# A decoder block on one core: the recurrent cell's first operand beside the last latent unit, and expert inputs by scattered rows

## The chip, the cores and the metric

One core of a Trainium2 chip runs one program, a whole decoder block. The metric is the device time of one execution in microseconds (us), the median of several runs. All data are float32, apart from a few bfloat16 helpers. PE is the matrix engine, DVE, ACT and POOL the three engines that work on rows, SP the engine whose queue issues most loads.

## The reference, cut to what matters

The input x has 2 batch entries of 1024 rows with 256 columns. Six layers follow one another: linear attention with a feed-forward part, latent cross-attention, a recurrent cell, causal self-attention with 16 heads, cross-attention to 64 context rows, and a mixture of experts. The change touches the seams of the cell and of the experts.

```python
# recurrent cell: scans over the two batch entries, 1024 rows each
def step(c, xt):
    ft = sigmoid(xt @ wf.T + c @ uf.T + bf)
    it = sigmoid(xt @ wi.T + c @ ui.T + bi)
    gt = tanh(xt @ wc.T + c @ uc.T + bc)
    return ft * c + it * gt, None
c_final, _ = lax.scan(step, c0, x)          # c0 = in_c, the same for every row
h = tanh(einsum('tbi,oi->tbo', x, wo) + c_final @ uo.T + bo)
...
x = x + cell(layernorm(x))
x = x + causal_attention(layernorm(x))
x = x + cross_attention(layernorm(x), context)
x = x + experts(layernorm(x))
```

The experts' layer takes 8 groups of 256 rows. Each row goes to its two best experts of 8, into one of 64 places that each expert has in each group; a row that finds no place is dropped. An expert computes `gelu(v @ w0) * (v @ w1) @ wo` on its 8 x 64 rows, with a hidden width of 1368, and each row's output is the sum of its two experts' rows weighted by the gates.

## The kernel before, in words

The residual x stays in SBUF as 16 tiles of 128 rows. Matmuls need operands with features on the partitions, so each layer normalises rows (statistics on DVE, the reciprocal root `rs_y` on POOL, the application on DVE at line L183), transposes the result on PE, and copies it out of PSUM on DVE or ACT. Layers are separate stages on PE. Inside most stages the order of instructions is written by hand (generators that are advanced in turn, or a list of step names like `CROSS_ORDER`); each engine then executes its own instructions strictly in that order. A few stages are ordered by a scheduler instead.

**Latent attention.** Four units (two of each batch entry) are attended one after another in 18 steps each. `Latent.run` advances, in each step, the attention of unit u (`attend`) and one step of a side generator (`side`). With unit 2 the side generator is `finish(0)`; unit 3 has none. PSUM holds three score buffers `s` of 128x1024 here. After unit 3 comes `finish(1)`, which ends with the output matmuls (L1046) and the additions to x (L1054).

**Recurrent cell.** `recurrent_cell` normalises all four groups of 512 rows (`norm_rows`, transposes at L192, copies at L123 and L125), then makes the bias of the first step's gates, `gb`: as the start state is the same vector `in_c` for every row, its product with each gate's matrix is one column (12 matmuls 128x1 at L1137, additions at L1144). Then come the gates of scan step 0 (L1158, 24 matmuls of 512 columns), those of step 1, and the output projection of each row tile, the second half beside the start of causal attention.

**Cross-attention.** `CROSS_ORDER` interleaves four units of 512 rows (`norm`, `turn`, `proj`, `max`, `sc`, `exp`, `os`, `out`, ...) with the routing of units 0 to 2 (`route_...`: statistics of x, normalised rows xn, transposes at L2062, router product at L2070), with the choice of experts for batch entry 0 (`choose_0`), and with four of the one-hot matrices (`ones`). The routing of unit 3 and `choose` for batch entry 1 follow in `Experts.run_in`.

**Experts.** In `run_in` rows are dispatched with matmuls: for each group of 256 rows, DVE makes for each 128-row tile a one-hot matrix `dm` of 128x512 (8 experts x 64 places, L2158 and L2159), and PE multiplies the rows xn with it (L2206, 64 records of 512 columns). ACT and DVE copy the results (L2215, L2219) into `pair`, the operands of all eight experts. Then each expert runs 11 chunks of hidden columns (`hidden`: 8 records each at L2266, gelu on ACT at L2274, product on DVE at L2275) and its output matmuls (L2281). Outputs of experts 0 to 5 are stored to rows in DRAM (`eo_rows`) and gathered later by 32 indirect transfers of POOL's queue (L2299) beside the last two experts; outputs of experts 6 and 7 are combined by matmuls with `cT`. Weights w0 and w1 (`load`) and wo (`load_out`) of an expert come by SP's queue, two experts ahead and at the expert's start.

## Time and the profile before

| what | us |
|---|---|
| median of 3 runs (1740.96 to 1742.96) | 1742.32 |
| the profiled execution | 1744.03 |
| its span on the core | 1742.2 |
| PE busy | 1657.0 |
| DVE, ACT, POOL busy | 807.3, 515.3, 263.5 |
| end of the latent outputs to the first gate record | 575.2 to 596.43 |
| gates of step 0 | 596.43 to 621.56 |
| cross-attention's last output matmuls end | 1225.7 |
| first up record of expert 0 | 1273.44 |
| gather transfers on POOL, 32 | 31.7 busy |

The profile is of one execution; its own time is that of its span and 1.8 us around it. A row of PE's timeline gives start, length and number of records of a run of matmuls, and in brackets the idle time ahead of it with what ended that. One logical float32 matmul leaves two records.

### The profile page before, as it was taken

The numbers are of one execution on the slowest core, as the hardware profiler recorded it, in microseconds if no ns is written. First come the engines' busy times: TensorE is split into PE (matmuls) and PEld (weight loads), VectorE is DVE, ScalarE is ACT, GpSimd is POOL, SyncE is SP. The second block draws the span as 40 slices with busy tenths as digits, with TensorE's granted clock in tenths as the row PEclk, the third lists the DMA queues.
The fourth block names the chain that finished last, engine by engine and source line by source line (L and its number), as shares of the span: only waits on it lengthen the run. The fifth ranks groups of instructions, "written<-read, shape, count | busy, mean of one in ns | idle before, by whom it ended". The sixth has DMA issues, their size and how long they took to land. (4 is left out here: it accounts for less than half of the span.)

```text
span 1742.2 us, 20929 instructions
## 1 busy us (share of the span) xinstructions
PE 1657.0 (95%) x8679; PEld 873.8 (50%) x8686; DVE 807.3 (46%) x1458; ACT 515.3 (30%) x872; POOL 263.5 (15%) x294
## 2 busy tenths in 40 slices
PE   7998899999999799999999999888899999999998
PEld 5746454343433547433433433556546655665466
DVE  8515237556542424476667668367621221111332
ACT  2321331432234123245555455433121111111110
POOL 2001140441223101113111112220000000000420
PEclk9999999999999799989999999999899999999999
DMA  6000000000000100100000000130003311332321
GB/s 230 1 3 1 0 3 1 1 0 1 1 1 0 36 1 1 32 1 1 1 2 1 1 1 2 53 146 2 1 0 109 108 66 45 109 109 71 101 67 49
DMA packets 30549, 59.15 MB, mean 34 GB/s; under 512 B 3640, under 2 KB 23672, under 8 KB 30072
## 3 DMA queue, kind: packets, MB, share of 16 engines
q1 hardware_dynamic: 25512, 50.46, 8.4%
q0 software_dynamic: 1536, 4.20, 0.9%
q10 hardware_dynamic: 3408, 3.17, 0.5%
q8 instruction: 68, 1.11, 0.3%
q14 instruction: 25, 0.20, 0.0%
HBM read 51.00 MB, written 6.82 MB: 33 GB/s over the span
## 5 line engine op out<-in xcount | busy, mean ns | idle before, releaser
L2266 PE MATMUL ps_s<-pair,w 128*128 128x512 f32 (+1 forms) x704 | 304.8, 592 | 0.2 <-ACT pair L2215 0.2
L2266 PEld LDWEIGHTS ps_s<-pair,w 128*128 128x128 f32 (+1 forms) x704 | 130.9, 187 | 164.4 <-issue 163.3
L1455 ACT ACTIVATE pT<-ps_t 128x512 f32<-128x512 f32 (+3 forms) x344 | 150.7, 490 | 145.3 <-PE ps_t L1420 143.0
L1345 PE MATMUL ps_s<-kT,qT 32*128 32x512 f32 (+3 forms) x768 | 178.1, 553 | 11.2 <-DVE part L1361 7.2
L2275 DVE TENSOR_TENSOR hid<-ga,ps_s 128x512 f32<-128x512 f32 (+1 forms) x88 | 60.5, 687 | 272.7 <-ACT ga L2274 272.7
L1420 PE MATMUL ps_t<-qT,kT 32*128 32x512 f32 (+3 forms) x688 | 181.8, 547 | 2.2 <-ACT pT L1455 2.2
L2281 PE MATMUL ps_o<-wo,hid 128*128 128x256 f32 (+1 forms) x704 | 153.6, 379 | 0.0
L1361 DVE TENSOR_REDUCE part<-ps_s 128x2 f32<-128x1024 f32 (+3 forms) x128 | 130.5, 1024 | 43.6 <-PE ps_t L1420 37.3
L2281 PEld LDWEIGHTS ps_o<-wo,hid 128*128 128x128 f32 (+1 forms) x704 | 133.8, 190 | 22.0 <-issue 4.1
L2274 ACT ACTIVATE ga<-ps_s 128x512 f32<-128x512 f32 (+1 forms) x88 | 52.5, 597 | 246.5 <-PE ps_s L2266 246.4
L1345 PEld LDWEIGHTS ps_s<-kT,qT 32*128 32x128 f32 x768 | 59.8, 189 | 87.0 <-issue 43.6
L1027 ACT ACTIVATE pT<-ps_s 128x1024 f32<-128x1024 f32 x64 | 65.5, 1024 | 115.9 <-PE ps_s L1020 115.9
L1385 PE MATMUL ps_o<-pT,vr 128*32 128x256 f32 (+4 forms) x1408 | 97.9, 356 | 1.8 <-POOL pT L1413 1.5
L1413 POOL TENSOR_SCALAR_AFFINE_SELECT pT<-pT 128x256 f32<-128x256 f32 x128 | 52.0, 408 | 313.3 <-ACT pT L1455 305.6
L2299 POOL DMA_INDIRECT found<-eo_rows,index x32 | 31.7, 992 | 422.7 <-DMA eo_rows<-rows 388.1
L915 DVE TENSOR_REDUCE part<-ps_s 128x2 f32<-128x1024 f32 x64 | 76.4, 1218 | 28.4 <-PE ps_s L908 27.7
L1353 DVE TENSOR_TENSOR ps_s<-ps_s,causal 128x256 f32<-128x256 f32 x128 | 55.0, 430 | 63.7 <-PE ps_t L1420 42.9
L1032 POOL TENSOR_TENSOR acc<-acc,pT 128x1024 f32<-128x1024 f32 x24 | 59.4, 2477 | 160.0 <-ACT pT L1027 157.3
L1385 PEld LDWEIGHTS ps_o<-pT,vr 128*32 128x32 f32 x1408 | 28.8, 108 | 97.9 <-issue 84.0
L1420 PEld LDWEIGHTS ps_t<-qT,kT 32*128 32x128 f32 x688 | 69.7, 188 | 10.7 <-ACT pT L1455 7.0
L908 PE MATMUL ps_s<-kT,qT 64*128 64x512 f32 x256 | 71.5, 639 | 0.8 <-DVE part L898 0.6
L947 PE MATMUL ps_o<-pT,vr 128*64 128x512 f32 x256 | 68.9, 619 | 0.9
(387 smaller groups left out, 2254.7 us busy)
## 6 DMA issues: line engine op xcount, KB each, us to landing
w<-in_w SPq DMA_DIRECT2D x32, 684.0 KB, 7.3
wo<-in_wo SPq DMA_DIRECT2D x8, 1280.0 KB, 6.8
eo_rows<-rows ACTq DMA_DIRECT2D x12, 256.0 KB, 4.6
w_ffn<-in_w_ffn SPq DMA_DIRECT2D x1, 2304.0 KB, 14.8
x<-in_x SPq DMA_DIRECT2D x4, 512.0 KB, 4.9
w<-in_w_cell SPq DMA_DIRECT2D x2, 1024.0 KB, 16.5
out_x<-x SPq DMA_DIRECT2D x8, 256.0 KB, 2.2
w<-in_w_lat SPq DMA_DIRECT2D x2, 768.0 KB, 16.2
```

Of the source, the lines that this page charges most:

```text
L908: nc.tensor.matmul(s3[:, hh, :], lhsT=q[rows, qt * P : (qt + 1) * P], rhs=kt[rows, half * 512 : (half + 1) * 512], start=True, stop=True,)
L915: nc.vector.tensor_reduce(part[:, half, qt, :], s3, AX.X, ALU.max, negate=True)
L947: nc.tensor.matmul(self.o[hh * 64 : hh * 64 + 64, :], lhsT=self.vr[b][:, kk, h * 64 : (h + 1) * 64], rhs=pT[:, hh, :], start=first, stop=last,
L1027: nc.scalar.activation(pT, s3, AF.Exp)
L1345: nc.tensor.matmul(s3[:, hh, :n], lhsT=q[rows, qt * P : (qt + 1) * P], rhs=kt[rows, at : at + n], start=True, stop=True,)
L1361: nc.vector.tensor_reduce(out, s3[:, :, :n], AX.X, ALU.max, negate=True)
L1385: nc.tensor.matmul(self.o[hh * 32 : hh * 32 + 32, cols], lhsT=vr[:, kk, 4 * grp + hh, :], rhs=pts[hh // 2][:, hh % 2, cols], start=first, ...
L1420: nc.tensor.matmul(out, lhsT=kt[rows, kk * P : (kk + 1) * P], rhs=q[rows, j * 512 + q0 : (j + 1) * 512], start=True, stop=True,)
L1455: nc.scalar.activation(pT[:, hh, q0:], heads[hh][:, q0:], AF.Exp)
L2266: nc.tensor.matmul(s[:n, i * 512 : (i + 1) * 512], lhsT=wt[:, kc, at : at + n], rhs=v[:, kc, :], start=(kc == 0), stop=(kc == DC - 1),)
L2275: nc.vector.tensor_mul(hid[:n, hc, :], ga[:n], s[:n, 512:])
L2281: self.k.nc.tensor.matmul(o, lhsT=hid[:n, hc, st * P : (st + 1) * P], rhs=to[:n, hc, :], start=(hc == 0), stop=(hc == len(HCH) - 1),)
```

## The change

**Cell.** `recurrent_cell` becomes a class. The operand of batch entry 0 (the norms of groups 0 and 1) and `gb` are made by `cell.ahead()`, which is the side generator of latent unit 3. `gb` is made in another form: six matmuls with `in_c` as the stationary side give one row of 768, ACT copies it out, and six matmuls 1x1 turn it back into columns. The norms of groups 2 and 3 are steps beside the gates of scan step 0.

**Experts.** Only experts 0 and 1 are still dispatched with matmuls, with one-hot matrices of 128 columns (`ones`, `disp`, and ACT copies `put`). Those of batch entry 0 are in `CROSS_ORDER`. For experts 2 to 7, POOL's queue scatters the rows of xn with 32 indirect transfers to rows in DRAM, which SP's queue fills with zeros beforehand (8 transfers of 393 KB behind those of `eo_rows` and ahead of wo of expert 0). For each of these experts, POOL's queue fetches its rows with 8 transfers of 64 rows, and 8 transposes and an ACT copy (`turned`) make the operand, ahead of the output matmuls of the expert before. Expert 0's up matmuls run in two halves of 256 columns. The first half, which needs batch entry 0 alone, is interleaved by hand (`FIRST_ORDER`) with the routing of unit 3, `choose` of batch entry 1 and its dispatch; the second half follows.

**Cross order.** `CROSS_ORDER` is another list of the same steps, with the new ones merged in.

```diff
-    def run(self, late):
+    def run(self, late, following):
...
+            if u == 3:
+                side = following
...
-def recurrent_cell(k, x, wt, pool):
-    xT = pool.tile([P, DC, B * N], F32, tag="xT", bufs=1, name="xT")
-    for g in range(NT // 4):
-        xh = norm_rows(k, pool, x, g)
-        k.feature_major(lambda i: xh[:, i, :], xT[:, :, g * 512 : (g + 1) * 512])
-    gb = pool.tile([P, 3, DC], F32, tag="gb", bufs=1, name="gb")
...
                 nc.tensor.matmul(
-                    o[:, 0:1],
-                    lhsT=w[u][:, kc, mc * P : (mc + 1) * P],
-                    rhs=k.vec("in_c", kc),
-                    start=(kc == 0),
-                    stop=(kc == DC - 1),
-                )
-            nc.vector.tensor_add(gb[:, gi, mc : mc + 1], o[:, 0:1], k.vec(bias, mc))
...
+class Cell:
...
+    def norm(self, g):
+        k, nc = self.k, self.k.nc
+        rows = lambda i: self.x[:, 4 * g + i, :]
+        mv, r = k.ln_stats(rows, 4)
+        yield
+        xh = self.rows()
+        for i in range(4):
+            k.ln_apply(xh[:, i, :], rows(i), mv, r, i)
+        yield
+        s = k.s()
+        for kc in range(DC):
+            for i in range(4):
+                at = (kc * 4 + i) * P
+                nc.tensor.transpose(s[:, at : at + P], xh[:, i, kc * P : (kc + 1) * P], k.ident)
+        dst, half = self.xT[g // 2], g % 2 * 512
+        nc.vector.tensor_copy(dst[:, 0, half : half + 512], s[:, :512])
+        nc.scalar.copy(dst[:, 1, half : half + 512], s[:, 512:])
+        yield
+    def first(self):
...
+        row = self.rows().rearrange("p t d -> p (t d)")[0:1, : 3 * D]
+        s = k.s()
+        for gi, (_, u, _) in enumerate(self.GATES):
             for kc in range(DC):
                 nc.tensor.matmul(
+                    s[0:1, gi * D : (gi + 1) * D], lhsT=k.vec("in_c", kc), rhs=self.w[u][:, kc, :],
+                    start=(kc == 0), stop=(kc == DC - 1),
+                )
+        nc.scalar.copy(row, s[0:1, : 3 * D])
+        yield
+        s = k.s()
+        for i in range(3 * DC):
+            nc.tensor.matmul(
+                s[:, i : i + 1], lhsT=row[:, i * P : (i + 1) * P], rhs=k.ones_row[:, 0:1], start=True, stop=True
+            )
+        self.gb = self.pool.tile([P, 3, DC], F32, tag="gb", bufs=1, name="gb")
+        at = VEC["bf"][0]
+        nc.vector.tensor_add(
+            self.gb.rearrange("p g m -> p (g m)"), s[:, : 3 * DC], k.vecs[:, at : at + 3 * DC]
+        )
+        yield
+    def ahead(self):
+        yield from self.first()
+        for g in range(2):
+            yield from self.norm(g)
...
-                    pairs = [(w[wn], xT[:, kc, step * N + nb * 512 : step * N + (nb + 1) * 512], kc) for kc in range(DC)]
+                    pairs = [(w[wn], self.xT[step][:, kc, cols], kc) for kc in range(DC)]
...
-        state = new
-        if step == 0:
-            continue
-        for t in range(NT):
-            rows = slice((t % TB) * P, (t % TB + 1) * P)
-            lhs = [xT[:, c, t * P : (t + 1) * P] for c in range(DC)] + [state[:, c, rows] for c in range(DC)]
-            o = k.t()[:, :D]
-            for c, a in enumerate(lhs):
-                nc.tensor.matmul(
-                    o, lhsT=a, rhs=w["uo" if c >= DC else "wo"][:, c % DC, :], start=(c == 0), stop=(c == len(lhs) - 1)
-                )
-            h = pool.tile([P, D], F32, tag="h", bufs=3, name="h")
-            nc.vector.tensor_add(h, o, k.row("cell_bo"))
-            nc.scalar.activation(h, h, AF.Tanh)
-            nc.vector.tensor_add(x[:, t, :], x[:, t, :], h)
-            yield t == TB - 1
+    def scan(self, pool):
+        self.xT[1] = self.operand(pool)
+        self.rows = lambda: pool.tile([P, 4, D], F32, tag="xh", bufs=2, name="xh")
+        side = chain(self.norm(2), self.norm(3))
+        for n, _ in enumerate(self.gates(pool, 0, None)):
+            next(side, None)
+        drain(side)
+        drain(self.gates(pool, 1, self.state))
...
+route_xT_1 sc_21 rows_3 route_prod_1 exp_21 route_copy_1 sc_31 choose_0 choose_0 sum_2 exp_31 choose_0
+choose_0 inv_2 spr_2 choose_0 val_2 choose_0 os_2 yT_2 choose_0 sc_30 choose_0 out_2 exp_30 ones_03
+ones_02 ones_01 ones_00 disp_00 add_2 route_stat_20 sum_3 put_00 ones_07 ones_06 ones_05 val_3 inv_3
+ones_04 spr_3 os_3 route_stat_21 disp_01 yT_3 route_mean_2 put_01 out_3 route_root_2 route_norm_20
+route_norm_21 add_3 route_turn_2 route_xT_2 route_prod_2 route_copy_2
...
-            elif name == "ones":
-                moe.ready[args[0]] = moe.dispatch(args[0])
+            elif name in ("ones", "disp", "put"):
+                getattr(moe, name)(*args)
...
+FIRST_ORDER = """
+up_06 route_stat_30 up_08 gelu_06 route_stat_31 route_mean_3 mul_06 route_root_3 gelu_08 mul_08 up_04
+route_norm_30 route_norm_31 route_turn_3 gelu_04 mul_04 route_xT_3 route_prod_3 up_01 route_copy_3
+choose_1 choose_1 choose_1 gelu_01 choose_1 up_00 choose_1 mul_01 choose_1 gelu_00 mul_00 up_0a choose_1
+choose_1 up_05 gelu_0a ones_12 ones_13 up_07 gelu_05 ones_10 ones_11 mul_0a gelu_07 disp_10 mul_07
+mul_05 up_02 put_10 ones_15 ones_16 ones_14 up_09 gelu_02 ones_17 mul_02 disp_11 gelu_09 mul_09 up_03
+put_11 gelu_03 mul_03
+"""
...
+        self.rows_in = [self.scratch.tile([AWAY + E * ROOM, D], F32, name=f"xi_rows{g}") for g in range(G)]
+        for g in range(G):
+            nc.sync.dma_start(
+                out=self.slots_of(g)[:, 2:, :], in_=zero[:C].unsqueeze(1).to_broadcast([C, E - 2, D])
+            )
...
-    def dispatch(self, t):
-        dm = self.pool.tile([P, E * C], F32, tag="dm", bufs=4, name="dm")
+    def ones(self, b, i):
+        nc, t = self.k.nc, b * TB + i
+        dm = self.ready[t] = self.pool.tile([P, 2 * C], F32, tag="dm", bufs=4, name="dm")
         nc.vector.tensor_single_scalar(dm, self.iota, s1, op=ALU.is_equal)
         nc.vector.scalar_tensor_tensor(dm, self.iota, s2, dm, ALU.is_equal, ALU.add)
+    def disp(self, b, h):
+        tb = self.placed = self.k.t()
+        for g in range(2):
+            for mc in range(DC):
+                at = (g * DC + mc) * 2 * C
+                for half in range(2):
+                    t = b * TB + 4 * h + 2 * g + half
+                    self.k.nc.tensor.matmul(
+                        tb[:, at : at + 2 * C], lhsT=self.xn[:, t, mc * P : (mc + 1) * P], rhs=self.ready[t],
+                        start=(half == 0), stop=(half == 1),
+                    )
+    def put(self, b, h):
+        t4 = self.placed.rearrange("p (g m e c) -> p g m e c", g=2, m=DC, e=2)
+        for g in range(2):
+            self.k.nc.scalar.copy(
+                self.xin[:, :, :, 4 * b + 2 * h + g, :].rearrange("p e m c -> p m e c"), t4[:, g]
+            )
+    def scatter(self, pool):
...
+        for half in range(2):
+            for i in range(2):
+                for g in range(G):
+                    t = 2 * g + half
+                    nc.gpsimd.indirect_dma_start(
+                        self.rows_in[g], bass.IndirectOffsetOnAxis(ap=rows[i][:, t : t + 1], axis=0),
+                        self.xn[:, t, :], None,
+                    )
+    def fetch(self, e):
+        if e >= E:
+            return
+        xr = self.fetched[e] = self.hp.tile([P, G // 2, D], F32, tag="xr", bufs=2, name="xr")
+        for g in range(G):
+            h = g % 2 ^ (e == E - 1)
+            self.k.nc.gpsimd.dma_start(out=xr[h * C : (h + 1) * C, g // 2, :], in_=self.slots_of(g)[:, e, :])
+    def turned(self, e):
+        k, xr = self.k, self.fetched.pop(e)
+        s = k.s()
+        for kc in range(DC):
+            for i in range(4):
+                at = (kc * 4 + i) * P
+                k.nc.tensor.transpose(s[:, at : at + P], xr[:, i, kc * P : (kc + 1) * P], k.ident)
+        v = self.inputs[e] = self.hp.tile([P, DC, 512], F32, tag="xe", bufs=2, name="xe")
+        k.nc.scalar.copy(v, s.rearrange("p (c n) -> p c n", c=DC))
...
-        xin = [pool.tile([P, 2048], F32, tag="pair", bufs=4, name="pair") for _ in range(E // 2)]
-        of = lambda ep: xin[ep].rearrange("p (e m g c) -> p e m g c", e=2, m=DC, g=G)
-        eo = pool.tile([P, G // 2, 2, D], F32, tag="eo", bufs=1, name="eo")
-        with tc.tile_pool(name="moe_route", bufs=1) as fp:
-            k.tiny = fp
-            for _ in chain(self.scores(3, fp), self.choose(1, fp)):
...
-            for g in range(G):
-                s = k.s()
-                for half in range(2):
-                    t = 2 * g + half
-                    dm = self.ready.pop(t) if t in self.ready else self.dispatch(t)
-                    for mc in range(DC):
-                        nc.tensor.matmul(
-                            s[:, mc * 512 : (mc + 1) * 512],
-                            lhsT=xn[:, 2 * g + half, mc * P : (mc + 1) * P],
-                            rhs=dm,
-                            start=(half == 0),
-                            stop=(half == 1),
-                        )
...
-                for ep in range(E // 2 - 1):
-                    nc.scalar.copy(
...
-                for i in range(2):
-                    nc.vector.tensor_copy(of(E // 2 - 1)[:, i, :, g ^ i, :], s4[:, :, MOST + i, :])
+    def run(self, out):
+                    route, choose = self.scores(3, fp, 1), self.choose(1, fp)
+                    self.begin(0)
+                    for step in FIRST_ORDER.split():
...
+                        elif name in ("up", "gelu", "mul"):
+                            getattr(self, name)(*args, n=4 * C)
+                        else:
+                            getattr(self, name)(*args)
+                    self.scatter(pool)
+                    for hc in range(len(HCH)):
+                        self.hidden(0, hc, 4 * C, 4 * C)
+                    self.fetch(2)
+                    self.fetch(3)
...
+                if e:
+                    self.begin(e)
+                    for hc in range(len(HCH)):
+                        self.hidden(e, hc)
+                if e:
+                    self.turned(e + 1)
+                    self.fetch(e + 3)
...
                 if e == 1:
-                    cT = self.combine(pool)
+                    cT = self.combine(hp)
             with tc.manual_schedule():
-                gather = self.gather(pool)
+                gather = self.gather(hp)
                 for i in range(2):
-                    for n, (hid, to) in enumerate(hidden(MOST + i)):
-                        for _ in range(2 if i or n > 2 else 0):
+                    self.begin(MOST + i)
+                    for hc in range(len(HCH)):
+                        self.hidden(MOST + i, hc)
...
+                    if not i:
+                        self.turned(E - 1)
...
+    def up(self, e, hc, first=0, n=512):
+        at, m = HCH[hc]
+        s = self.now[hc] = self.k.s()
+        for i, wt in enumerate(self.loaded[e]):
+            for kc in range(DC):
+                self.k.nc.tensor.matmul(
+                    s[:m, i * 512 : i * 512 + n],
+                    lhsT=wt[:, kc, at : at + m],
+                    rhs=self.inputs[e][:, kc, first : first + n],
+                    start=(kc == 0),
+                    stop=(kc == DC - 1),
+                )
+    def hidden(self, e, hc, first=0, n=512):
+        self.up(e, hc, first, n)
+        self.gelu(e, hc, n)
+        self.mul(e, hc, first, n)
...
+    cell_pool = ctx.enter_context(ExitStack())
+    first = cell_pool.enter_context(tc.tile_pool(name="cell_x", bufs=1, reuse_waits="tile"))
+    cell = Cell(k, x, w_cell, first, lambda: early.tile([P, 4, D], F32, tag="xh", bufs=1, name="xh"))
...
-            latent.run(late)
+            latent.run(late, cell.ahead())
...
-            cell, start = recurrent_cell(k, x, w_cell, pool), causal.start()
-            while not next(cell):
-                pass
-            for _ in start:
-                next(cell, None)
-            for _ in cell:
-                pass
+        with k.banks("ps_e", 2, 4, 0), tc.tile_pool(name="cell", bufs=1, reuse_waits="tile") as pool:
+            with tc.manual_schedule():
+                cell.scan(pool)
+            for t in range(TB):
+                cell.out(pool, t)
+            for t, _ in zip_longest(range(TB, NT), causal.start()):
+                if t is not None:
+                    cell.out(pool, t)
+        cell_pool.close()
```

## The prediction

> **What bounds the kernel now.** I read the page's engine table and slices first (PE is busy 95% of the span, so only its idle time, its slow-clock time and its work are worth anything), then the chain of waits (PE holds it nearly throughout), then the table of windows around the three places that the diff touches, and last PE's timeline inside them. The windows, with columns busy us (instructions) for each engine, then granted clock, DMA share, GB/s:
>
> ```profile
> 500.00:566.00 66.00, 65.85 (x355) 21.37 (x356) 24.20 (x29) 26.52 (x28) 23.09 (x12) 1.00 0.00 1
> 576.00:597.00 21.00, 12.32 (x57) 11.04 (x58) 13.08 (x46) 3.63 (x5) 3.02 (x3) 0.55 0.22 75
> 597.00:622.00 25.00, 25.00 (x54) 10.75 (x53) 5.47 (x8) 8.25 (x12) 0.00 (x0) 0.90 0.00 1
> 1186.00:1234.00 48.00, 42.07 (x424) 31.34 (x423) 31.13 (x86) 15.46 (x19) 2.02 (x2) 0.93 0.01 1
> 1234.00:1273.40 39.40, 35.56 (x106) 18.16 (x106) 25.84 (x87) 8.28 (x26) 1.01 (x1) 0.88 0.00 1
> 1273.40:1311.50 38.10, 38.06 (x89) 16.75 (x90) 8.52 (x18) 7.79 (x13) 0.00 (x0) 1.00 0.02 4
> ```
>
> The last latent unit (first row) has no idle PE; the cell's entry (second) has 8.7 us of it and half a clock; the end of cross-attention and the dispatch (fourth, fifth) lose 9.8 us and run at 0.93 and 0.88; expert stages are full. PE's timeline shows what fills the second and fifth stretch:
>
> ```profile
> 577.02 1.24 PE L192 MATMUL ps_t<-ident,xh 128*128 128x128 f32 x8 [1.84 <-DVE xh L183]
> 584.88 1.94 PE L192 MATMUL ps_t<-ident,xh 128*128 128x128 f32 x8 [3.52 <-DVE xh L183]
> 589.83 0.66 PE L192 MATMUL ps_t<-ident,xh 128*128 128x128 f32 x2 [3.01 <-DVE xh L183]
> 593.16 3.41 PE L1137 MATMUL ps_t<-vecs,w 128*128 128x1 f32 x16
> 596.43 25.29 PE L1158 MATMUL ps_t<-xT,w 128*128 128x512 f32 x52
> ...
> 1218.54 7.17 PE L1928 MATMUL ps_s<-w,yT 128*128 128x256 f32 x32 [0.48 <-ACT os L1881]
> 1227.44 1.64 PE L2062 MATMUL ps_s<-ident,w 128*128 128x128 f32 x8 [1.73 <-DVE w L183]
> 1230.18 3.58 PE L2070 MATMUL ps_t<-router,xT 128*128 128x8 f32 x16 [1.10 <-ACT xT L2065]
> 1237.62 0.45 PE L2062 MATMUL ps_s<-ident,w 128*128 128x128 f32 x1 [3.86 <-DVE w L183]
> ...
> 1252.13 20.85 PE L2206 MATMUL ps_s<-dm,w 128*128 128x512 f32 x48
> 1273.44 1.98 PE L2266 MATMUL ps_s<-pair,w 128*128 128x512 f32 x4 [0.24 <-ACT pair L2215]
> ```
>
> PE waits for DVE's normalised rows (xh, w), not for a transfer; and 48 one-hot matmuls stand in a row although nothing but copies hangs on them. One logical f32 matmul is two records. Full-speed starts are 0.43 us apart at 512 columns (20.85/48), 0.22 at 256 (7.17/32), 0.109 for a 128-column transpose (0.87/8).
>
> **Part 1, the cell.** Removed from PE's path: from the latent output's last record (575.2) to the first gate record at 596.43, 21.2 us. Of it remains DVE's last residual add, 1.22 us, which the gates don't read, but which stands ahead of the work of norm(2); I keep 1.3 us. So −19.9. The 52 gate records would take 52 x 0.43 = 22.5 us and took 25.29; behind a busy PE they start at speed: −2.8. [...] I take 2.8, from the trace.
>
> Added to PE: norms 2 and 3 beside step 0's gates, 16 transposes x 0.109 = 1.75 (their DVE chain has 22 us of gates to hide in; its last copies are needed only by step 1). Beside latent unit 3: six 1x256 logical matmuls, 12 x 0.216 = 2.6; six 1x1 ones, 12 records, between 12 x 0.11 (choose's 32-column records between 1247.75 and 1248.88, ten in 1.13 us) and 12 x 0.21 (the 16 records of L1137 in 3.41 us) — I take the upper, 2.5, as its row is the same form; 16 transposes, 1.75. That stretch is PE-bound (first window row), so all 6.9 us count. DVE's side work there (8 stats, 8 applies at 0.34, copies 0.69: about 10 us) fits into the 41.8 us that DVE idles in those 66; ACT's copies (0.69 each, one 1x768 row about 0.8, an estimate from the 128x512 copies) fit beside 26.5 busy of 66. POOL gains two rs_y of 1.0 us; its acc adds (2.4 us each for every other step) have slack of about 2 us a step. If that cover failed, each late acc would stall the finish, up to 3 us once.
> Sum: −19.9 − 2.8 + 1.75 + 6.9 = **−14** (between −10 and −17).
>
> **Part 2, experts.** From out_3's end (1225.75) to expert 0's last up record (1311.47) it was 85.7 us. After:
> - turn_2, xT, prod_2: DVE now normalises unit 2 ahead of add_3, so the 1.73 us wait goes; 8 x 0.109 = 0.9, the wait for ACT's xT 1.1, prod 1.85 (the 16 records of 1244.07): 4.1, with 1 us for imperfection 5.1.
> - FIRST_ORDER: half of expert 0's ups, 88 records x 0.216 = 19.0; turn_3 and prod_3 2.7; choose's ten records 1.1; disp_10 and disp_11, 32 records x 0.109 = 3.5. Together 26.3. Stalls, with two s buffers and a strict order: xT_3 1.3, norm of unit 3 0.7, up_07 behind mul_0a, which stands behind the ones on DVE, about 3, two changes of ACT's table between exponential and gelu at 1.28: 5 to 8. I take 7.
> - The second half of the ups: 19.0.
> Sum 57.4: −28.3. The removed r_st wait (DVE 5.60 us behind prod_2) stays as it is, but PE now has ups in front of it, where before it had the 3.86 us of idle.
> - Added elsewhere: `turned` for experts 2 to 7, 48 transposes x 0.109 = 5.2, all on a full PE (its ACT copy of 1.01 us has the 19 us of the outs to hide in); disp_00 and disp_01 inside the cross order, 3.5, of which about 1 fills an existing wait: +2.5. The 40 copies of dispatched rows (24 ACT, 16 DVE) were hidden and are worth nothing.
> - The new CROSS_ORDER: same PE work, 12.4 us of idle in 1126 to 1234. I see no row that says which order is better: between −4 and +4, taken as 0. Each wait that it shifts is of 1 us or less.
> Sum: −28.3 + 5.2 + 2.5 = −20.6; **−20**, rounded down for the orders' small waits.
>
> **What the new queue work hides behind.** POOL gets 32 indirect scatters and 48 fetches, and SP eight zero fills (3.1 MB). No row shows a scatter or a POOL fetch. The nearest is the indirect gather, of the same size, which starts every 1.25 us:
>
> ```profile
> 1629.12 0.94 POOL L2299 DMA_INDIRECT found<-eo_rows,index  x1 [0.30 <-issue]
> 1630.37 0.95 POOL L2299 DMA_INDIRECT found<-eo_rows,index  x1 [0.30 <-issue]
> ...
> found<-eo_rows,index POOLq DMA_INDIRECT x32, 2.8
> ```
>
> Counted from out_3's end: slots of unit 3 are there at about +38; 32 x 1.25 = 40 gives +78; the eight fetches of expert 2 +88, landed 2.8 later, +91. They are first read by turned(2), ahead of expert 1's outs: 57 + 19 (outs) + 38 (ups of 1) = +114. Slack 23 us over 40 transfers. Later fetches have one or two 57 us expert periods. Behind the scatter on POOL stand only these fetches and the gather, which starts two experts before its reader. POOL computes nothing in the expert stages (x0 in the window row). So nothing, above; below, no gain either, as nothing waits for POOL now. The zero fills go behind both weight loads of the experts, and ahead of wo(0), first read near +57; at the 143 GB/s that this stretch moves they are 22 us: hidden.
>
> [...] By the row, the gathers keep their 0.95 us while DVE multiplies beside them (hid reads PSUM) and adds x. In these stages DVE is busy 8.5 of 38.1 us: [...] I take the row.
>
> **Total.** −14 − 20 = −34. Against the profiled execution: span 1742.2 to 1708, and with the 1.8 us around it 1710. The runs' median, 1742.32, lies 1.7 below that execution's 1744.03: **1708 us**.
>
> **Rivals.**
> - A, slower: POOL's chain is late. Place: PE waiting for xe at expert 2's first up (or turned(2)). It costs nothing until a transfer takes 1.25 + 23/40 = 1.8 us; it cancels the gain at 1.25 + (23 + 34)/40 = 2.7; [...] Against: the gather rows. 0.04.
> - B, the FIRST block and the new cross order stall: two s buffers, one written-out order across four engines, and an ACT that changes tables. Some 10 us more: 1718. For it: DVE is the busiest waiting partner already (25.84 of 39.4). 0.14.
> - C, unit 3 doesn't absorb the cell's side work: an s buffer kept by a side step stalls the score matmuls by about 1 us in each of eight steps: 1716. For it: three s buffers, PE bound. Against: ACT and DVE idle over half there. 0.10.
> - D, the clock stays up and the cross order fills more of its 12.4 us and of the slow-clock 5: another 12 us off, 1696. 0.09.
> - E, cell steps are not early at all: the order is written by hand, so only a wait on a buffer could hold them; w_cell has been loaded long before. 0.01, about 1722.
> - The forecast itself: 0.62, its own range 1701 to 1715.
>
> The range reaches from D to between B and the worst of both, 1694 to 1722. A measurement of this kernel can tell about 0.2%, 3.5 us, from no change. Only A, or B and C with twice their price, come near 1739: faster 0.95, same 0.02, slower 0.03.
>
> **What would show it.** PE's gap between the last latent output and the first gate: 21 us to under 3, with the gates' 52 records in about 22.5 us; unit 3 longer by about 7 us. From out_3's end to the end of the ups 57 us rather than 86, without L2206's row of 48. turned about 0.9 us a time with no idle in front of it. POOL's scatters every 1.25 us, and no DMA among the releasers of PE or of turned. Wrong, if PE waits for xr or xe, if a scatter takes 2.7 us, or if the FIRST block takes over 43 us.

## The result, and the profile after

The changed kernel takes **1725.38 us** (median of 4 runs, 1722.54 to 1727.68) where the kernel before takes 1742.64 (1740.96 to 1743.59): ratio 0.9901, 95% interval 0.9884 to 0.9918. It is faster by 17 us, half of the forecast 34, and lies 3 us above the stated range. The profiled execution has a span of 1723.4 us, 18.8 less than before.

The table cuts both spans at the same events on PE. "Forecast" is what the prediction's terms give for that stretch.

| stretch on PE | before | after | change | forecast |
|---|---|---|---|---|
| start to the last latent output record | 575.2 | 585.3 | +10.1 | +6.9 |
| to the first gate record | 21.2 | 1.3 | −19.9 | −19.9 |
| gates of scan step 0 | 25.1 | 26.5 | +1.4 | −1.05 |
| gates of step 1 | 39.5 | 39.5 | 0 | 0 |
| cell output and causal start | 48.4 | 46.6 | −1.8 | 0 |
| causal stage, first score to first cross record | 416.7 | 422.6 | +5.9 | 0 |
| cross stage, to the end of out_3 | 99.6 | 107.9 | +8.3 | +2.5 |
| routing of the last unit, dispatch, ups of expert 0 | 85.8 | 58.5 | −27.3 | −28.3 |
| outs of expert 0 and the rest | 430.7 | 435.2 | +4.5 | +5.2 |
| span | 1742.2 | 1723.4 | −18.8 | −34.65 |

The matrix engine's clock is either full or half in these traces. At half clock its records took close to twice as long: of the gates of step 0 in the kernel before, 7 records ran in the 5 us from 597 on, at a clock of 0.51, and 13 in the next 5 us, at 1.00. Where half-clock time is given a cost below, it is half of that time, an estimate from these counts. The granted clock's mean over the span is 0.976 in both, with 82 us at half clock before and after. The gap, the gates and the cell's output shed 27.3 us of that (18.4, 5.5 and 3.4) and the last stretch of routing and dispatch 3.5; the causal stage takes on 20.5, the cross stage 6.9, and unit 3 3.4.

The two stretches that the change was about came out close to what was worked out. The windows show what came beside it (columns as in the prediction: busy us and instructions of PE, weight loads, DVE, ACT, POOL, then granted clock):

```profile
510.00:575.60 65.60, 63.49 (x331) 21.31 (x329) 26.54 (x45) 24.93 (x27) 20.89 (x10) 0.97 0.00 1
585.30:613.10 27.80, 25.88 (x68) 11.65 (x69) 16.07 (x37) 10.60 (x15) 7.61 (x6) 1.00 0.18 62
1186.00:1229.70 43.70, 41.09 (x426) 29.71 (x426) 30.16 (x92) 14.74 (x20) 3.04 (x3) 0.96 0.00 1
1229.70:1270.00 40.30, 37.49 (x193) 32.27 (x192) 19.96 (x76) 12.02 (x23) 1.01 (x1) 0.87 0.00 1
1270.00:1288.00 18.00, 18.00 (x85) 15.58 (x84) 5.23 (x17) 3.84 (x10) 13.17 (x14) 1.00 0.23 91
```

The cell's entry (585 on) runs at full clock without the 8.7 us of idle time. The last row is the second half of expert 0's ups, full, with POOL's scatters beside it (13.17 us busy). But unit 3 (first row) now has 2 us of idle PE, which it had not. PE's timeline at the places that the prediction quoted:

```profile
537.93 1.64 PE L1150 MATMUL ps_s<-ident,xh 128*128 128x128 f32 x8 [1.97 <-DVE xh L183]
...
586.59 5.42 PE L1201 MATMUL ps_t<-xT,w 128*128 128x512 f32 x12 [1.31 <-DVE x L1054]
592.27 1.73 PE L1150 MATMUL ps_s<-ident,xh 128*128 128x128 f32 x8 [0.26 <-DVE xh L183]
...
1231.65 2.67 PE L2151 MATMUL ps_t<-router,xT 128*128 128x8 f32 x16 [1.10 <-ACT xT L2146]
1234.17 8.10 PE L2407 MATMUL ps_s<-xin,w 128*128 128x256 f32 x24
...
1267.29 20.89 PE L2407 MATMUL ps_s<-xin,w 128*128 128x256 f32 x96
1288.01 18.31 PE L2434 MATMUL ps_o<-wo,hid 128*128 128x256 f32 x84
```

PE waits 1.31 us for DVE's last residual add and then starts the cell's gates, as forecast. The transposes of norms 2 and 3 take 1.7 us a group rather than 0.9. Expert 0's first ups run at 1234, 39 us earlier than before, and nothing stands between its last ups and its outs. The POOL queue, which the slower rival was about:

```profile
1272.41 0.97 POOL L2277 DMA_INDIRECT xi_rows<-w,row  x1 [0.30 <-issue]
...
1310.46 0.96 POOL L2277 DMA_INDIRECT xi_rows<-w,row  x1 [0.31 <-issue]
1311.42 2.19 POOL L2290 DMA_DIRECT2D xr<-xi_rows  x4
...
1343.92 1.04 PE L2299 MATMUL ps_s<-ident,xr 128*128 128x128 f32 x8
```

A scatter takes 0.96 us and starts every 1.27, a fetch takes 0.5. Expert 2's first 8 fetches are issued by about 1317; the transposes that read them run at 1343.92 without waiting. The gather row was the right measure, and rival A did not happen.

### The profile page after: what moved, and what is told of

Read it like the earlier page. It is cut to its first block, busy times and chain, and to the rows that moved or that the text cites. A ratio compares the mean times of both kernels' runs of the same rounds, so it can differ in the third digit from the quotient of the medians.

```text
span 1723.4 us, 21309 instructions
## 1 busy us (share of the span) xinstructions
PE 1647.6 (96%) x8815; PEld 885.6 (51%) x8822; DVE 804.0 (47%) x1454; ACT 522.5 (30%) x876; POOL 319.6 (19%) x376
## 4 chain that ended last, share of the span: by engine, by line
PE 80%; DVE 11%; issue 5%; ACT 2%; POOL 1%; DMA 0%; ACTq 0%; POOLq 0%; DVEq 0%
PE ps_s L2407 18%; PE ps_o L2434 9%; PE ps_s L1396 8%; PE ps_o L1436 5%; PE ps_s L1020 4%; PE ps_t L1355 4%; PE ps_o L947 3%; PE ps_t L1201 3%; PE ps_t L1471 2%; PE ps_s L908 2%; PE ps_t L539 2%; PE ps_s L822 2%; PE ps_s L381 2%; DVE part L915 1%; PE ps_f L556 1%
## 5 line engine op out<-in xcount | busy, mean ns | idle before, releaser
L2407 PE MATMUL ps_s<-xe,w 128*128 128x512 f32 (+1 forms) x528 | 229.0, 592 | 0.0
L1396 PE MATMUL ps_s<-kT,qT 32*128 32x512 f32 (+3 forms) x768 | 182.9, 574 | 10.0 <-DVE part L1412 6.2
L1471 PE MATMUL ps_t<-qT,kT 32*128 32x512 f32 (+3 forms) x688 | 185.6, 557 | 2.2 <-ACT pT L1506 2.2
L2422 DVE TENSOR_TENSOR hid<-ga,ps_s 128x512 f32<-128x512 f32 (+2 forms) x99 | 62.0, 628 | 266.4 <-ACT ga L2418 266.3
L2407 PEld LDWEIGHTS ps_s<-xe,w 128*128 128x128 f32 (+1 forms) x528 | 98.0, 187 | 121.3 <-issue 120.0
L2418 ACT ACTIVATE ga<-ps_s 128x512 f32<-128x512 f32 (+2 forms) x99 | 54.4, 550 | 245.3 <-PE ps_s L2407 244.0
L2407 PE MATMUL ps_s<-xin,w 128*128 128x256 f32 (+3 forms) x264 | 81.7, 471 | 0.5 <-DVE hid L2422 0.5
L1020 PE MATMUL ps_s<-qT,kT 64*128 64x512 f32 x256 | 70.2, 625 | 0.2 <-DVE part L915 0.2
## 6 DMA issues: line engine op xcount, KB each, us to landing
w<-in_w_cell SPq DMA_DIRECT2D x2, 1024.0 KB, 16.5
```

The costliest lines, as they stand in the source:

```text
L1020: nc.tensor.matmul(s3[:, hh, :], lhsT=self.ones_h[hr, :] if i else kt[hr, kk * P : (kk + 1) * P], rhs=rows[hr, cols] if i else q[hr, cols] ...
L1396: nc.tensor.matmul(s3[:, hh, :n], lhsT=q[rows, qt * P : (qt + 1) * P], rhs=kt[rows, at : at + n], start=True, stop=True,)
L1471: nc.tensor.matmul(out, lhsT=kt[rows, kk * P : (kk + 1) * P], rhs=q[rows, j * 512 + q0 : (j + 1) * 512], start=True, stop=True,)
L2407: self.k.nc.tensor.matmul(s[:m, i * 512 : i * 512 + n], lhsT=wt[:, kc, at : at + m], rhs=self.inputs[e][:, kc, first : first + n], start=( ...
```

## The experiments

Times of experiments are medians, each beside runs of the kernel before on the same chip; ratios are to those. "Stage" lengths are read from one profiled execution each, between the events of the table above. That execution need not be typical: executions of one file differ in time and in the clock that they were granted, the 21 of experiment 1 from 1730.06 us (clock 0.986) to 1741.44 (0.977).

**1. The cell's part alone** (the kernel before with the class `Cell`, its side steps in unit 3 and `scan`; nothing of the experts):

> The kernel before with the cell's part alone (operand of entry 0 and first bias beside latent unit 3, norms of entry 1 beside the gates); experts and cross order as before. In the changed kernel this part had gained 10.2 us by the start of the causal scores (709.42 to 699.19), and the causal stage then lost 5.9 of it (430.4 us instead of 424.5 from the first projection to the first cross record), with the same instructions at a lower granted clock. Theory: the loss in the causal stage is a half-clock stretch that any execution may have, so alone the part gives 10 us: about 1732. Rival: the earlier start itself brings on the slow stretch, then only 4: about 1738.

1739.34 us against 1743.62, ratio 0.9968 (0.9957 to 0.9979). The causal stage took 422.6 us here too, with the same 46.6 in front of it. So the median is the rival's number: alone, the part gives 4 to 6 us, and in the trace it brings the longer causal stage with it, without any change of the experts or the cross order. The trace is of the longest of the 21 executions, though. Four took 1730.06 to 1733.55 us at a clock of 0.985 to 0.986, which is the theory's gain of 10 us and more: not every execution pays the clock's price. In which stage those four were shorter, no trace shows.

**2. The cell's part undone** (the changed kernel with `recurrent_cell`), run on the same chip as the changed kernel itself (`after_again`, 1723.9 us, ratio 0.9905, 0.9875 to 0.9934):

> The changed kernel with the former cell (experts and cross order as changed). The cell's part was worth 4 us by the difference of the causal stage's end (1126.15 to 1121.79), so this takes 4 to 5 us more than the changed kernel run beside it, and its causal stage takes 416.7 us again, not 422.6. Rival: the causal stage's length varies by itself; then it takes 10 us more and the stage has 422.6.

1729.04 us, ratio 0.9938 (0.9917 to 0.9958): 5.1 us more than the changed kernel, and a causal stage of 416.7 us. Both are as the theory had it, and the mirror image of experiment 1. The stage's length is the firmer part: with four executions each, the two times overlap (1723.47 to 1730.22, and 1720.91 to 1728.69). The traced execution is the shortest of the four; up to the last latent output it took 569.4 us where the kernel before took 575.2 for the same instructions, with 3.4 us at half clock against 13.7. The cell's early start saves 20 us of gap, and some 5 us are left of it.

**3. The former cross order**, with the new steps set in behind its last choose_0:

```diff
 CROSS_ORDER = """
-text_0 stat_31 norm_00 norm_01 stat_30 turn_00 bias_0 turn_01 vals_0 text_1 ...
+text_0 norm_01 norm_11 norm_00 stat_21 turn_01 bias_0 turn_00 vals_0 text_1 ...
...
+inv_2 choose_0 exp_31 choose_0 spr_2 choose_0 sum_3 ones_03 yT_2 val_3 inv_3 ones_02 spr_3 os_3
+ones_01 yT_3 ones_00 out_2 add_2 disp_00 ones_07 ones_06 put_00 ones_05 ones_04 route_stat_20
+route_stat_21 out_3 route_mean_2 disp_01 route_root_2 put_01 route_norm_20 route_norm_21 add_3
+route_turn_2 route_xT_2 route_prod_2 route_copy_2
```

> The changed kernel, but with the former cross order up to the last choose_0 and the new steps (ones, disp, put) set in behind it. Theory: the new order itself costs about 5 us (its stretch from the first cross record to the end of out_3 is 107.9 us against 99.6, of which disp is 3.5), so this one gives about 1720. Rival: the merged steps hold up the end of the stage under any order: 1725, as the changed kernel.

The first run gave 1746.47 us, which is neither (ratio 1.0013, 1.0002 to 1.0024), although its cross stage took 101.5 us, less than the 103 that the theory comes to. What ate it is seen in PE's timeline, 14 us after the first scatter:

```profile
1281.61 3.67 PE L2408 MATMUL ps_s<-xin,w 128*128 128x256 f32 x8 [2.79 <-issue]
1290.09 3.71 PE L2408 MATMUL ps_s<-xin,w 128*88 128x256 f32 x8 [4.82 <-DVE hid L2423]
1293.60 5.39 PE L2435 MATMUL ps_o<-wo,hid 128*128 128x256 f32 x20
1301.10 0.38 PE L2435 MATMUL ps_o<-wo,hid 128*128 128x256 f32 x1 [2.11 <-issue]
1303.89 0.59 PE L2435 MATMUL ps_o<-wo,hid 128*128 128x256 f32 x1 [2.42 <-issue]
```

All but one of these waits of PE are for nothing that the profile shows ("issue"); ACT's gelu (once 17.1 us after ACT's work before it) and SP's weight loads (45.3 us after the first scatter, 16.5 in the changed kernel) are late too; soon after the last scatter (1304.57) it ends. All three kernels with scatters that were traced on this chip had it: from out_3 to the first ups of expert 1 they took 24 to 26 us longer than on the others. Repeated on another chip:

> old_order once more. Its 1746 came from a chip on which three variants stood still for about 27 us beside the scatters. Theory: the stall belongs to that chip, so on another one this kernel takes 6 us less than the changed kernel, about 1718; if it lands on the same chip, 1746 again. Rival: the stall belongs to this kernel's edits: 1746 anywhere.

1719.08 us, ratio 0.9859 (0.984 to 0.9879). The same file is 27 us slower on the one chip than on the other, so the stall goes with the chip (or with how the program lay there) and not with an edit. Its cause was not found. A wait for instructions, the rival of experiment 4, finds no support: in 75 us around the scatters the queue that loads instructions moved two packets, 0.03 MB in all, and took 0.2% of the time of the DMA engines, with the stall as in the changed kernel without it. And the cross order's own cost is read: the cross stage and the stretch behind it together take 162.7 us under the former order and 166.4 under the new one; in the trace of `after_again`, the new order again, 169.6, with 6.8 us more at half clock. (They are taken together because disp_01 stands behind out_3 in the former order.)

> The changed kernel itself, unaltered. Three variants of it took 1746 to 1752, 20 us more than it; in their traces PE, ACT and SP stand still for some 27 us in all while POOL scatters the rows, from about 14 us after the first scatter to the last one, which the changed kernel's trace does not show. Theory: the stall depends on the chip (where the rows and the program lie), not on the edits, so the changed kernel has it here too: about 1750. Rival: the edits shifted something into it, and the changed kernel stays at 1725.

The 1723.9 of `after_again` came from a chip that showed no stall, so it does not decide between the two; the repeat of the former order does.

**4. Half of the scatters:**

> The changed kernel with half of the scatters (the rows of the second choice are left out, so experts 2 to 7 get only part of their rows). Theory: the other engines are held up while the scatters run, so with 16 of them, over 20 us after their start, at most some 6 us of stall are left: about 1729 where the changed kernel takes 1750 on the same chip. Rival: the stall is a matter of where in the program it is (a wait for instructions), and stays.

1721.82 us (1712.32 to 1728.89), ratio 0.9876, on the chip without the stall. It therefore tells nothing about it. The stages in which the scatters run were of the same length with 16 as with 32 (58.5 us from out_3 to the end of expert 0's ups, and 435.2 from there to the end, in both): where they do not stall, scatters cost nothing that these traces show. That the scatters bring on the stall on the other chip rests on their coincidence in time in three traces; it was not tried apart.

**5. One empty step between statistics and application of norms 0 and 1:**

> The changed kernel with one empty step between the statistics and the application of norms 0 and 1, so that DVE's application falls into a step in which DVE, not POOL, adds to acc. Theory: in the changed kernel DVE's four applications took 3.40 us instead of 1.38 because POOL's acc add (2.34 us) ran beside them and held them; PE idled 1.97 us and then ran at 0.60. Apart, the applications take 1.38 us, PE has no idle time there, unit 3 is 3 to 3.5 us shorter: about 1722. Rival: it was rs_y, late on POOL, that held DVE; then the stall comes back in the later step: 1725.

1751.8 us, ratio 1.0059, on the chip with the stall; its time says nothing, its trace does. Unit 3, from the first side record to the last output, took 66.78 us instead of 64.36: worse. Each add to acc reads what the one before it wrote, so DVE's add came only after POOL's, and the application of norm 0 again fell beside an add of POOL and took 3.40 us again; PE waited 1.12 and 1.96 us. The edit missed its aim, and says nothing against the theory that POOL's add holds DVE up.

**6. POOL's adds taken away from DVE's applications** (on top of the former cross order; one of the two lines in each kernel):

```diff
-                        add = nc.gpsimd if n % 2 else nc.vector
+                        add = nc.gpsimd if n % 2 and (u, j, n) != (3, 0, 3) else nc.vector   # dve_acc
+                        add = nc.gpsimd if n % 2 and (u, j) != (3, 0) else nc.vector         # dve_acc2
```

> The changed kernel with the former cross order (new steps set in behind the last choose_0) and with one of unit 3's adds to acc on DVE instead of POOL, the one that ran beside the application of norm 0. [...] without POOL's add beside it DVE's application takes 1.38 us, not 3.40, PE has no 1.97 us wait in unit 3 and no slow clock behind it: 3 us less there; with the 6.4 us that the former order saved in the cross stage, 9 us less than the changed kernel beside it. Rival: rs_y comes late anyway and PE waits as before: only the 6.4.

> The changed kernel with the former cross order and all adds to acc in the first half of latent unit 3 on DVE. In dve_acc the application of norm 0 took 1.38 us as forecast, but that of norm 1 then ran beside POOL's next add and took 3.44. [...] with no POOL add beside either, both take 1.38 us, PE's waits for xh in unit 3 (3.2 us there) go below 1 us, and unit 3 is some 3 us shorter than in the changed kernel; about 1714 with the former order. Rival: DVE itself gets too full, and PE waits for it elsewhere in unit 3.

DVE's applications and POOL's work beside them in the changed kernel, DVE first:

```profile
535.35 3.40 DVE L183 TENSOR_SCALAR xh<-x,ln_mv,rs_y 128x256 f32<-128x256 f32 x4 [1.13 <-POOL rs_y L144]
547.15 1.38 DVE L183 TENSOR_SCALAR xh<-x,ln_mv,rs_y 128x256 f32<-128x256 f32 x4
```

```profile
535.30 2.34 POOL L1032 TENSOR_TENSOR acc<-acc,pT 128x1024 f32<-128x1024 f32 x1
542.97 2.35 POOL L1032 TENSOR_TENSOR acc<-acc,pT 128x1024 f32<-128x1024 f32 x1 [5.33 <-ACT pT L1027]
545.27 1.01 POOL L144 TENSOR_TENSOR rs_y<-ln_ve,minus_half 128x4 f32<-128x4 f32 x1
548.27 2.48 POOL L1032 TENSOR_TENSOR acc<-acc,pT 128x1024 f32<-128x1024 f32 x1 [1.98 <-DVE xh L183]
```

and in `dve_acc2`, DVE:

```profile
535.91 1.38 DVE L183 TENSOR_SCALAR xh<-x,ln_mv,rs_y 128x256 f32<-128x256 f32 x4 [0.91 <-POOL rs_y L144]
545.66 1.38 DVE L183 TENSOR_SCALAR xh<-x,ln_mv,rs_y 128x256 f32<-128x256 f32 x4 [0.90 <-POOL rs_y L144]
```

Four applications take 1.38 us alone, and 2 us more when an add of POOL, 2.34 us long, began 0.05 us before them: the first of the four then ends 0.14 us after the add does, and the other three follow at their usual pace. In `dve_acc` it happened to the last application of norm 1 (3.44 us for the four, PE waiting 2.06) and no longer to norm 0. With no add beside either, both are short. In each of these cases the application that began beside a running add of POOL ended only after it; by what the two are kept apart was not shown. The prediction looked at POOL's transfers beside DVE (0.95 us for a gather, and 0.96 for a scatter in the changed kernel), and not at POOL's adds, where the delay was.

It is worth little all the same: unit 3 shrank to 63.82 and 63.21 us from 64.36, 1.2 us at most where 3 was expected. PE's waits for xh are no shorter, 2.0 us in the changed kernel, 2.9 in `dve_acc` and 2.1 in `dve_acc2`; what is gone is the 3.41 us at half clock behind the first of them, worth some 1.7 us. The wait stayed because the root `rs_y` became late instead, as the first rival said. In `dve_acc2`, POOL's and PE's rows:

```profile
533.96 1.92 POOL L144 TENSOR_TENSOR rs_y<-ln_ve,minus_half 128x4 f32<-128x4 f32 x1 [15.88 <-DVE ln_ve L168]
...
536.47 1.64 PE L1150 MATMUL ps_s<-ident,xh 128*128 128x128 f32 x8 [0.85 <-DVE xh L183]
546.22 1.64 PE L1150 MATMUL ps_s<-ident,xh 128*128 128x128 f32 x8 [1.25 <-DVE xh L183]
```

`rs_y` takes 1.92 us here, and 1.01 in the changed kernel: the add that went to DVE (1.22 us) begins 0.17 us before it, in `dve_acc` too (1.92 us), and now POOL is the one that is held up.

`dve_acc` took 1716.03 us (ratio 0.9856, 0.9834 to 0.9878), `dve_acc2` 1718.81 (0.987, 0.9853 to 0.9886). Against `after_again` on the same chip, `dve_acc` is 7.9 us faster, and the ranges of their runs do not meet (1713.73 to 1717.67, and 1720.91 to 1728.69). By the two traces that is not unit 3: of 8.6 us, 6.0 lie in the causal stage (416.6 us against 422.6) and 3.1 in the cross stage and what follows it.

**7. The causal stage's clock.** Filling the waits in the maxima of the first causal unit with repeated matmuls:

```diff
-            for hh in range(2):
+            for hh in (0, 1, 0, 1)[: 2 if u or n > 256 else 4]:
```

> The changed kernel with the score matmuls of up to 256 columns in the causal maxima of the first unit issued twice (the second writes the same values), where PE waits for DVE's reductions. Theory: these short waits bring the granted clock down (0.5 to 0.7 for 40 us in the changed kernel); filled, it stays up and the causal stage loses 6 us or more, to about 1718. Rival: the clock falls for another reason, and the stage stays; the repeats cost under 2 us: 1725 to 1727.

1746.97 us, ratio 1.0022, on the chip with the stall; the causal stage took 422.8 us. As a whole the stage is no shorter, so the forecast failed. The theory is neither borne out nor refuted: the stage's half-clock time fell from 41.0 us to 30.7, and the first transposes of the attention's output come 4.0 us earlier in the stage than in the changed kernel, in spite of 32 more records; then a stretch of 10.24 us at half clock near the stage's end, which the changed kernel does not have, took it back. The repeats also moved the stage's first gap, so filling and moving cannot be told apart.

Then the place of the gap, by throwaway matmuls ahead of the last gate of step 0 (three, and one):

```diff
+                    if step == 0 and nb == 1 and mc == 1 and gi == 2:
+                        for _ in range(3):
+                            nc.tensor.matmul(o, lhsT=pairs[0][0][:, 0, mc * P : (mc + 1) * P],
+                                             rhs=pairs[0][1], start=True, stop=True)
                     for n, (wm, rhs, kc) in enumerate(pairs):
```

> The changed kernel with three throwaway matmuls of 512 columns (six records, 2.6 us of PE) ahead of the last gate of scan step 0. Theory: the trace's half-speed stretches all start and end on one grid of 3.41 us, and what a gap costs depends on where it lies in the grid. In the causal stage the first stretch starts 2.99 us after PE's first gap in the changed kernel and lasts 23.89 us, but 3.71 us after it and 6.83 us long in the kernel before. 2.6 us more work in front gives 2.99 - 2.6 + 3.41 = 3.8 us: the causal stage takes 416.7 us again, not 422.6, and the useless work makes the kernel 3 us faster, about 1721. Rival: the cell's change slows the causal stage through something else; then it stays at 422.6 and the time is 1727.

> As extra3, with one throwaway matmul (0.86 us). The stretch would start 2.13 us after the gap. Theory: any causal length between 416.7 and 422.6 or somewhat above can follow, but not that of extra3 and of the changed kernel both; most likely a slow first stretch still, 422 us or more. Rival: 422.6, as without it.

1726.26 us (ratio 0.9918, 0.9893 to 0.9943) with three, 1725.39 (0.9901, 0.987 to 0.9933) with one. No gain in time, so that forecast failed. But the causal stage moved the way the theory says: 418.8 us with three (416.7 was forecast), 425.4 with one. The trace keeps the stretches in which the granted clock was half; every one within the program is 3.41 us or a multiple, and so, in the traces of the kernel before and the changed one, is the full-clock time between two of them (3.41 to 341.3 us). In the causal stage:

| kernel | first stretch begins after PE's first gap, us | it lasts | half-clock time in the stage | stage |
|---|---|---|---|---|
| dve_acc | 3.25 | 6.83 | 20.5 | 416.6 |
| cell_undone | 3.66 | 6.83 | 20.5 | 416.7 |
| before | 3.71 | 6.83 | 20.5 | 416.7 |
| dve_acc2 | 3.86 | 6.83 | 27.3 | 418.8 |
| extra3 | 3.91 | 6.83 | 27.3 | 418.8 |
| apart | 3.96 | 6.83 | 27.3 | 418.8 |
| after, and 5 others with its cell | 2.99 to 3.12 | 23.89 | 41.0 | 422.6 |
| extra1 | 2.24 | 23.89 | 47.8 | 425.4 |

The stage's instructions are the same in all of these. Ahead of its first half-clock stretch PE has three short waits for DVE's reductions, 2.2 us in all; the stretch of the changed kernel begins at 724.11:

```profile
722.46 0.49 PE L1396 MATMUL ps_s<-kT,qT 32*128 32x128 f32 x4 [1.34 <-DVE part L1412]
723.52 0.49 PE L1396 MATMUL ps_s<-kT,qT 32*128 32x128 f32 x4 [0.57 <-DVE part L1412]
724.32 1.09 PE L1422 MATMUL ps_s<-ident,mneg 128*128 128x128 f32 x4 [0.31 <-DVE part L1412]
```

With 2.6 us of added work the stretch began 3.91 us after the gap (2.99 − 2.6 + 3.41 = 3.8 was worked out), it lasted 6.83 us instead of 23.89, and the stage became 3.8 us shorter. 0.86 us put it 0.75 us earlier, and it stayed long. The further 2.8 us of `extra1` come from elsewhere: a stretch of 10.24 us near the stage's end, as in `warm`. The windows show it, first of the changed kernel, then of the kernel before over the same work, 10 us later:

```profile
730.00:740.00 10.00, 9.39 (x36) 4.58 (x36) 6.77 (x8) 3.91 (x8) 1.23 (x3) 0.50 0.00 0
740.00:750.00 10.00, 9.03 (x36) 3.19 (x34) 5.81 (x7) 1.32 (x5) 1.22 (x3) 0.60 0.00 0
750.00:760.00 10.00, 9.32 (x76) 4.34 (x75) 7.16 (x15) 2.38 (x7) 1.23 (x3) 0.66 0.01 2
```

```profile
740.00:750.00 10.00, 8.77 (x42) 3.38 (x42) 8.86 (x9) 3.69 (x8) 1.63 (x4) 0.91 0.00 0
750.00:760.00 10.00, 8.13 (x58) 4.25 (x54) 7.30 (x13) 1.76 (x6) 1.22 (x3) 0.78 0.00 0
760.00:770.00 10.00, 9.87 (x88) 3.98 (x88) 7.03 (x12) 4.55 (x11) 1.70 (x5) 0.71 0.01 2
```

PE is busier in the first of these windows (9.39 us against 8.77), and gets less done (36 records against 42): the granted clock (third figure from the end) is 0.50, against 0.91. With 0.61 us of idle time against 1.23, the slow stretch does not stand out in the waits; only the clock column shows it.

## Why the prediction was wrong, point by point

- **The gap before the gates** (−19.9) was right in mechanism and size, and so were the 5.2 us for `turned` (4.5 for the whole tail). **FIRST_ORDER with the dispatch** (−28.3, measured −27.3) was right in size, partly by luck: of the 7 us set aside for stalls, PE waited 1.7, and lost some 4.4 to half clock (8.8 us of it), which the sum did not have. These steps carry the gain that there is.
- **The new CROSS_ORDER, "taken as 0"**, is the first failed step. The stage grew by 8.3 us where 2.5 was counted. The 2.5 were 3.5 us of dispatch less 1 us of waits that it fills. But PE's idle time grew, from 9.3 us to 10.9, and its half-clock time from 6.8 us to 13.7, which costs 3.4. Against the former order with the same new steps the new one costs 3.7 us in the profile and 5 to 6 in the runs (1719.08 against 1723.9 and 1725.38, on different chips). "Each wait that it shifts is of 1 us or less" does not hold: PE's first two long waits grew from 1.3 and 1.1 us (the second in two parts) in the kernel before,

```profile
1136.95 1.17 PE L1805 MATMUL ps_s<-keys,q 32*128 32x128 f32 x32 [1.32 <-ACT q L1797]
1143.32 0.49 PE L1805 MATMUL ps_s<-keys,q 32*128 32x128 f32 x4 [0.46 <-DVE q L1795]
1144.45 1.16 PE L1805 MATMUL ps_s<-keys,q 32*128 32x128 f32 x28 [0.64 <-DVE m L1816]
```

to 2.2 and 1.6 us in the changed one:

```profile
1132.72 1.42 PE L1856 MATMUL ps_s<-keys,q 32*128 32x128 f32 x32 [2.19 <-ACT q L1848]
...
1145.38 1.17 PE L1856 MATMUL ps_s<-keys,q 32*128 32x128 f32 x32 [1.57 <-DVE q L1846]
```

- **The causal stage, of which the prediction says nothing**, is the second: +5.9 us, or +4.1 with the slow stretch at the causal start that went. It charged clock loss only where the old profile showed it (2.8 us at the gates) and took the rest as fixed. The waits of this stage would not have led it there: the first gaps are short, 1.34, 0.57 and 0.31 us. But moving the work moved these gaps against the 3.41 us steps in which the clock changed (the first stretch began 2.99 us after the first gap, not 3.71, and lasted 23.89 us, not 6.83), in a stage that nobody touched. Experiments 1, 2 and 7 show it, in their traces.
- **Unit 3, "all 6.9 us count"**: +10.1. The 16 transposes were taken at 0.109 us each; they follow DVE's four applications, which end 0.33 us apart, so a group takes 1.3 to 1.6 us, not 0.9. And PE waited 1.97 us for an application that POOL's add held up, followed by one half-clock stretch of 3.41 us, which costs some 1.7. The prediction saw that DVE had 41.8 us of idle time, and not that an add of POOL could make four applications take 3.40 us instead of 1.38. One term erred the other way: the twelve records 1x1 took 1.49 us, not 2.5. The row behind the 2.5 (L1137) had run at a clock of 0.50.
- **Gates of step 0**: the 52 records ran at full clock (1.00) as forecast (12 in 5.42 us, 12 in 5.32, 28 in 12.18), but the norm groups cost 1.7 us each and 0.6 us of waits: +1.4 rather than −1.05.
- The misses add up to the difference between forecast and profile: unit 3 3.2, gates 2.45, causal stage and its start 4.1, cross stage 5.8, dispatch 1.0, the tail −0.7; together 15.85 us, which is 34.65 − 18.8. (A slip of addition, 0.9 + 1.1 + 1.85 given as 4.1 rather than 3.85, changes nothing; and the row of 48 records that the prediction calls 48 one-hot matmuls is 24.)
- **Rivals.** A was rejected, as the gather row had said. B was right for the cross order and wrong for FIRST_ORDER. C had the right place and the wrong mechanism: no side step held a score buffer, PE waited for the normalised rows. Both places cost at once, which the range left out; the clock of the causal stage was in none.

## What to carry to other kernels

Here PE was 95% busy, and a change that saved idle time also moved every later gap; what the clock made of those gaps was part of the price (5.9 us in the causal stage, with 20.5 us more at half clock). In such a kernel, leave several us either way for stages that are not touched, and read the clock column of all stages after the change. The transposes that were put beside a full PE cost the pace of their operands, not their own (1.3 to 1.7 us a group, not 0.9), and DVE and POOL, each idle for more than half of unit 3's window (26.5 and 20.9 us busy of 65.6), still held each other up (four applications 3.40 us instead of 1.38, `rs_y` 1.92 instead of 1.01). A written order is to be measured on its own before it is merged with other changes: here the former order with the new steps was the better one (1719.08 us). And a better time is not yet a better order: `dve_acc` (1716 us) beats both kernels, but by its trace mostly through the clock in the causal stage, at which nobody had aimed.

## What the runs showed of the hardware that was not expected

- Half-clock stretches lasted 3.41 us or a multiple, up to 23.89 us in one piece with PE 97% busy. No single long gap stood ahead of that one, only waits of 1.34, 0.57 and 0.31 us within 3.2 us. In thirteen traces of the same causal instructions, a first stretch that began 3.25 us or more after PE's first gap lasted 6.83 us, and one that began 3.12 us or less after it lasted 23.89. The stage took 416.6 to 418.8 us with the short one and 422.6 to 425.4 with the long one. The place was the same (2.99 to 3.12) in six traces of kernels with the same cell; why it is not drawn anew in each is open. Executions without a trace did differ in their clock (0.977 to 0.986 in experiment 1).
- On one chip of three, PE, ACT, DVE and SP lost 24 to 26 us while POOL issued 32 indirect scatters, PE at times passing a single record of a matmul in 1.4 to 2.8 us; on another the same file ran without a wait. A gather of the same number of transfers in the kernel before had no such stall there (1743.62 us on that chip). Its cause is open.
- A 128x1024 add on POOL (2.34 us) that had begun first held up DVE's 128x256 applications by 2.0 us (3.40 and 3.44 us for four in the changed kernel and `dve_acc`, 1.38 alone), though both engines were idle more than half of that stage (DVE busy 26.5 us of 65.6, POOL 20.9, in the changed kernel). The other way round, an add of DVE that had begun first made POOL's 128x4 product `rs_y` take 1.92 us instead of 1.01, in `dve_acc` and `dve_acc2`.
